# A stack of four low-rank-adapted layers: first weights in pieces, a combined table for the last two layers, and shared last sums

## The chip, the cores and the metric

The kernel runs on one core of a Trainium2 chip. Its time is device microseconds of one execution of the program; three executions are shown, and their median counts. A profile is taken of a separate execution, and its times are microseconds from the start of the span. TensorE (PE) multiplies, VectorE (DVE), ScalarE (ACT) and GpSimd (POOL) do elementwise work, and DMA transfers are issued by SyncE (SP), ScalarE or GpSimd, each on its own queue.

## The reference

The input x has 8 sequences of 256 tokens with 1024 features, in float32. Four residual layers follow each other. Each has low-rank adapters of rank 16, selected per sequence by an index:

```python
# layer 0: x + x W^T + b + 2 * (x A0[i]) B0[i]
# layer 1: gate and up (1024 -> 2752), silu(gate) * up, down (2752 -> 1024),
#          each with an adapter of its own
    Bx = jnp.einsum('bni,bri->bnr', x, B_req)          # layers 2 and 3
    out = jnp.einsum('bnr,bor->bno', Bx, A_req)
    return out * SCALING
    ...
    x = x + _L2_cond_ref(x, L2_cond_A, L2_cond_B, itok_B_4_50)
    x = x + _L3_cond_ref(x, L3_cond_A, L3_cond_B, itok_B_3_7)
```

In layers 2 and 3 nothing but the low-rank part is added, with a factor of 1. With B2, A2, B3, A3 the selected tables of one sequence (the first of each pair going down to rank 16), the output is x + A2 B2 x + A3 B3 (x + A2 B2 x). So it is enough to form t2 = B2 x and t3 = B3 x + (B3 A2) t2, and to add A2 t2 + A3 t3 at the end.

## The kernel before

Activations lie transposed, features on the 128 partitions and tokens along them. The 2048 tokens are worked in two blocks of 1024, a block in two halves (`n`) of 512 tokens, and a half holds two sequences. A chunk is 128 features; x has eight (`NC`), and `arrival` orders them 0, 4, 1, 5, 2, 6, 3, 7. Large products use a seven-product scheme (sums of operands on DVE and GpSimd, seven block products on TensorE, sums of results on DVE), but the first output pair of layer 0 in block 0 is computed plainly, since it can start before any sums (`plain`).

The program is written as units, each a list of products, with hooks in slots before and inside them: `u.before(k, slot, f)` runs `f` k units earlier. Work with a cost can be put in a list, `beside`, which is emptied by shares at the slots of each unit; `need(key)` forces what stands under that key. A scheduler then settles waits and buffers; each engine runs its own instructions in the order in which they were written. Tiles of 8 KB per partition come from one pool of 22 (`big`), PSUM banks from four small pools (`ps_a` two, `ps_b` one, `ps_c` one, `ps_l` four).

**The start.** The kernel issues four small loads of indices (`ids`, L127) and one of the bias (L186) on ScalarE's queue. `load_w(0)` (L782) issues two weight tiles of 512 KB on SP, and `load_x` (L752) the chunks of x, 256 KB each, in turn on SP and ScalarE. DVE works out offsets from the indices (L131 to L202), with which GpSimd gathers adapter tables (L208). `sum_x` makes the sums of x for later units. `plain` (L822) then does, for each half of the tokens, eight chunks times two output tiles, followed by `first_shrink` (x times the gathered A0, L238) and `expand` (L253).

**Layers 2 and 3.** In the last layers each sequence has 16 ranks of layer 2 and 16 of layer 3. In a PSUM bank of 128 rows, rows 64n to 64n+31 hold B2 x and the next 32 rows B3 x, for the two sequences of half n; a mask zeroes, for each token, the ranks of the other sequence. `tables23` gathers the tables in the first unit of the down projection, on TensorE multiplies B3 with A2 (L1271, 16 products that give a 32 by 32 table per half), and places the results in a 128 by 128 table `ba` that is zero elsewhere. `shrink23` (L238) is done in parts, as chunks of the down projection's result become final. `last_layers` then runs shrink of the last chunks, `rank_out` (the mask, L231), the product with `ba` added to the same bank (L1314), `rank_out` again, and eight times two expand products (L1319, by L253), each followed by a DVE sum into the result (L1321) and a store of 256 KB on ScalarE's queue (L1325). In block 0 the stores are put into `beside`; in block 1 they are issued at once.

```python
            t = rank_out(ps, 1.0, f"t2_{blk}")
            nc.tensor.matmul(ps, st["ba"], t, start=False, stop=True, skip_group_check=True)
            t = rank_out(ps, 1.0, f"t23_{blk}")
```

Of the kernel before, what the change touches and what calls it, by code (L numbers as in the profile page):

```python
# [13 lines left out]
P = 128  # L14
# [30 lines left out]

SHARE = {1: 1.1, 2: 0.8, 3: 1.1, 5: 0.7, 6: 0.3, 7: 0.3, 4: 0.8}
SHARE_REST = {1: 0.5, 2: 0.3, 3: 0.5, 5: 0.3, 6: 0.2, 7: 0.2, 4: 0.3}
BIG = 2048
NBIG = 22

# [2 lines left out]
def kernel(  # L53
# [22 lines left out]
    a2s: bass.AP,  # L76
    bb2: bass.AP,
    bb3: bass.AP,
    outT: bass.AP,
):  # L80

# [39 lines left out]
    def bank(pool, name):  # L121
        return pool.tile([P, 512], F32, tag=pool.name, name=name)


    ids = const.tile([P, 4, NB], I32, tag="ids", name="ids")
    for j, tok in enumerate((tok0, tok1, tok2, tok3)):
        nc.scalar.dma_start(out=ids[:, j, :], in_=tok[None, :].to_broadcast([P, NB]))  # L127
    part = const.tile([P, 1], I32, tag="part", name="part")
    nc.gpsimd.iota(part, pattern=[[0, 1]], base=0, channel_multiplier=1)
    part_f = const.tile([P, 1], F32, tag="part_f", name="part_f")  # L130
# [52 lines left out]
        nc.vector.tensor_single_scalar(off_23[rows], off_23[rows], float(SLOTS2 * R), op=ALU.add)  # L183

    bias = const.tile([P, NC], F32, tag="bias", name="bias")
    nc.scalar.dma_start(out=bias, in_=b0)  # L186

# [552 lines left out]
    def layer0(blk):  # L740
        st = sts[blk]

        def load_x():
            st["x"] = xs = [[None] * NN for _ in range(NC)]
            t = {}
            for n in range(NN):
                for h in range(2):
                    t[n, h] = big(f"x_{blk}_{n}_{h}").rearrange("p (c t) -> p c t", c=HC)
                for i, k in enumerate(arrival):
                    xs[k][n] = t[n, k // HC][:, k % HC, :]  # L750
                    at = blk * TB + n * 512
                    (nc.sync, nc.scalar)[i % 2 if blk == 0 else 0].dma_start(  # L752
                        out=xs[k][n], in_=xT[k * P : (k + 1) * P, at : at + 512]
                    )
            st["a0"] = gather_a(a0, 0, blk, f"a0_{blk}")
            st["b0"] = gather_b(bb0, off_b[:, 0, blk : blk + 1], f"b0_{blk}")

# [13 lines left out]
        def x1(k, n):  # L771
            key = "x1", n, k % 2
            if key not in st:
                st[key] = big(f"x1_{blk}_{n}_{k % 2}").rearrange(
                    "p (i c t) -> p i c t", i=2, c=2
                )
            return st[key][:, k // HC, (k // 2) % 2, :]

        def load_w(o):
            t = big(f"w0_{blk}_{o}").rearrange("p (j k) -> p j k", j=2)  # L780
# [30 lines left out]

        def plain(o, at):

            p, x = o + HC, st["x"]
            pss = {}
            at(0)
            for n in range(NN):
                for j in (o, p):
                    pss[j, n] = bank((ps_a, ps_l)[n], f"pp_{blk}_{j}_{n}")
                for i, c in enumerate(arrival):  # L820
                    for j in (o, p):
                        nc.tensor.matmul(  # L822
                            pss[j, n],
                            st["w", o][:, j // HC, c * P : (c + 1) * P],
                            x[c][n],
                            start=i == 0,
                            stop=i == NC - 1,
                        )
# [49 lines left out]
        for i, o in enumerate((0, 2, 1, 3)):  # L878
            if blk == 0 and i == 0:
                u = Unit("0_plain", lambda at, o=o: plain(o, at), 0)  # L880
                u.before(1, 0, lambda o=o: load_w(o))
                u.before(1, 0, load_x)
                for c in range(HC):
                    u.before(1, 0, lambda c=c: sum_x(c))
            else:
                u = Unit(f"0_{blk}_{o}", lambda at, o=o: job(o, at), 1.3)
                u.before(1, 0, lambda o=o: load_w(o))
                u.before(1, 3, lambda o=o: sum_w(o))
                if i == 0:
# [235 lines left out]
    def down_projection(blk):  # L1125
# [133 lines left out]
        def tables23():  # L1259
            st["a23"] = gather_b(a23, off_23[:, blk : blk + 1], f"a23_{blk}")  # L1260
            st["b2"] = gather_a(bb2, 2, blk, f"bb2_{blk}")
            st["b3"] = gather_a(bb3, 3, blk, f"bb3_{blk}")
            a_s = gather_a(a2s, 2, blk, f"a2s_{blk}")


            v, w = (x.rearrange("p b (r c) -> p (b r) c", c=NC) for x in (a_s, st["b3"]))
            ps = bank(ps_l, f"pba_{blk}")
            for c in range(NC):
                for n in range(NN):
# [5 lines left out]
                        start=c == 0,  # L1275
                        stop=c == NC - 1,
                    )
            ba = st["ba"] = const.tile([P, P], F32, tag="ba", name=f"ba_{blk}")
            nc.gpsimd.memset(ba, 0.0)
            for n in range(NN):  # L1280
                rows, at = slice(64 * n, 64 * n + 32), 64 * n + 32
                nc.vector.tensor_scalar_mul(ba[rows, at : at + R], ps[rows, :R], even_f[rows])
                nc.vector.tensor_scalar_mul(
                    ba[rows, at + R : at + 2 * R], ps[rows, R : 2 * R], odd_f[rows]
                )

        def shrink23(chunks):

            for mh in range(2):
                for n in range(NN):  # L1290
                    need(("x2", blk, mh, n))
            if chunks[0] == 0:
                st["p23"] = bank(ps_l, f"p23_{blk}")
            for c in chunks:
# [13 lines left out]
        def last_layers():  # L1308
# [1 line left out]
            x2 = st["x2"]  # L1310
            shrink23([HC - 1, NC - 1])
            ps = st["p23"]
            t = rank_out(ps, 1.0, f"t2_{blk}")
            nc.tensor.matmul(ps, st["ba"], t, start=False, stop=True, skip_group_check=True)  # L1314
            t = rank_out(ps, 1.0, f"t23_{blk}")
            for o in range(NC):
                pss = [bank((ps_l, ps_a)[o % 2], f"p23_{blk}_{o}_{n}") for n in range(NN)]
                for n in range(NN):
                    expand(pss[n], st["a23"], o, t, 64 * n, 64 * n + 64, start=True)  # L1319
                for n in range(NN):  # L1320
                    nc.vector.tensor_add(x2[o][n], x2[o][n], pss[n])  # L1321
# [25 lines left out]
        for o in range(HC):  # L1347
# [4 lines left out]
            if o == 0:  # L1352
# [2 lines left out]
                u.before(1, 4, sum_h)  # L1355
                u.at(0, lambda: need(("hm", blk)))
                u.before(2, 5, tables23)
            else:
                u.at(5, lambda o=o: shrink23([o - 1, o - 1 + HC]))
        units[-1].at(9, last_layers)  # L1360
# [150 lines left out]
```

## Time and profile before

| | us |
|---|---|
| three executions | 1821.07, 1823.34, 1825.03 |
| median | 1823.34 |
| the profiled execution, its own time | 1823.25 |
| its span | 1821.5 |
| TensorE idle before its first product | 9.31 |
| first group of products (L822), from and to | 9.31 to 40.02 |
| start of the last expands (L253), block 1 | 1806.12 |
| last store landed | 1820.37 |

The span runs from the first to the last event that the profiler records. A float32 product is two records on TensorE, one a pass; a pass of 128 by 128 by 512 takes 0.43 us at full clock and 0.855 us at half. The column "granted clock" of a stretch is the mean of what the throttle allowed, 1.00 being full; the whole span has 0.994. The two ends of the span look so in windows (columns: from and to, length, then busy time and number of instructions of PE, PEld, DVE, ACT and POOL, granted clock, share of the 16 DMA engines, GB/s):

```
5.00:10.00 5.00, 0.69 (x1) 0.50 (x2) 0.10 (x2) 0.00 (x0) 0.00 (x0) 1.00 0.73 239
10.00:16.00 6.00, 6.00 (x9) 2.39 (x8) 5.33 (x33) 0.00 (x0) 4.08 (x5) 1.00 0.96 335
16.00:40.00 24.00, 24.00 (x60) 10.33 (x61) 10.18 (x16) 1.28 (x1) 17.85 (x19) 1.00 0.77 274
1806.00:1822.00 16.00, 9.35 (x32) 3.93 (x32) 9.72 (x17) 0.00 (x0) 0.00 (x0) 0.86 0.70 263
```

In the second row nine passes start in 6 us, each twice as long as those of the third row, though the clock column there shows 1.00; the length of the passes is the surer sign at the start.

### The profile page before, as it was taken

The numbers are of one execution on the slowest core, as the hardware profiler recorded it, in microseconds if no ns is written. First come the engines' busy times: TensorE is split into PE (matmuls) and PEld (weight loads), VectorE is DVE, ScalarE is ACT, GpSimd is POOL, SyncE is SP. The second block draws the span as 40 slices with busy tenths as digits, with TensorE's granted clock in tenths as the row PEclk, the third lists the DMA queues.
The fourth block names the chain that finished last, engine by engine and source line by source line (L and its number), as shares of the span: only waits on it lengthen the run. The fifth ranks groups of instructions, "written<-read, shape, count | busy, mean of one in ns | idle before, by whom it ended". The sixth has DMA issues, their size and how long they took to land.

```text
span 1821.5 us, 20497 instructions
## 1 busy us (share of the span) xinstructions
PE 1790.1 (98%) x7588; PEld 1310.4 (72%) x7588; DVE 1081.7 (59%) x1674; ACT 307.0 (17%) x548; POOL 1002.7 (55%) x773
## 2 busy tenths in 40 slices
PE   7999999999999999999899999999999999999998
PEld 3444477878787878788764578888878887888743
DVE  3674354776767575777852464666666668446623
ACT  0111022111111111233310031020202021222100
POOL 5302577887987677334650377675758573444300
PEclk9999999999999999999999999999999999999999
DMA  6376785767675756679741684575757565654302
GB/s 228 144 286 250 268 342 184 301 210 308 244 301 198 273 184 240 236 274 354 264 151 52 231 330 164 201 257 208 254 210 255 211 219 208 228 180 182 110 0 93
DMA packets 114707, 402.33 MB, mean 221 GB/s; under 512 B 12336, under 2 KB 42160, under 8 KB 105136
## 3 DMA queue, kind: packets, MB, share of 16 engines
q1 hardware_dynamic: 97920, 362.84, 54.4%
q0 software_dynamic: 10208, 27.67, 4.4%
q10 hardware_dynamic: 6480, 10.51, 1.6%
q8 instruction: 61, 1.00, 0.2%
q14 instruction: 38, 0.31, 0.0%
HBM read 316.56 MB, written 84.41 MB: 220 GB/s over the span
## 4 chain that ended last, share of the span: by engine, by line
PE 91%; DVE 7%; DMA 1%; issue 1%; ACT 0%; DVEq 0%; SPq 0%; ACTq 0%
PE pa L453 26%; PE pc L453 13%; PE pa L352 10%; PE pa_d L453 9%; PE pb L453 6%; PE pc_d L453 5%; PE pc L352 5%; PE pb L352 3%; PE pb_d L453 2%; PE pl L931 2%; PE pa_r L453 2%; PE pp L822 2%; PE pd L238 1%; PE pc_r L453 1%; PE p L238 1%
## 5 line engine op out<-in xcount | busy, mean ns | idle before, releaser
L453 PE MATMUL pa<-tk,sw 128*128 128x256 f32 x1120 | 268.8, 383 | 1.7 <-DVE c_X L484 1.7
L453 PE MATMUL pc<-tk,sw 128*128 128x256 f32 x1120 | 267.1, 382 | 0.0
L453 PEld LDWEIGHTS pa<-tk,sw 128*128 128x128 f32 x1120 | 209.1, 190 | 58.6 <-issue 11.4
L453 PEld LDWEIGHTS pc<-tk,sw 128*128 128x128 f32 x1120 | 213.9, 191 | 30.9 <-POOL w_B L414 0.8
L453 PE MATMUL pa<-tk,w_B 128*128 128x256 f32 x960 | 228.4, 381 | 0.2 <-DVE c_Y L487 0.2
L453 PEld LDWEIGHTS pa<-tk,w_B 128*128 128x128 f32 x960 | 181.2, 190 | 34.7 <-DVE c_E L484 6.5
L423 POOL TENSOR_TENSOR sw<-w_B 128x512 f32<-128x512 f32 x60 | 77.3, 1289 | 134.6 <-PE pa L453 118.8
L453 PE MATMUL pb<-tk,w_B 128*128 128x256 f32 x480 | 114.5, 382 | 0.0
L453 PE MATMUL pc_d<-dh_d,dw_d 128*128 128x256 f32 x448 | 103.6, 384 | 7.5 <-DVE c_d_X L487 5.7
L591 POOL TENSOR_TENSOR dx_d<-dw_d 128x1024 f32<-128x1024 f32 x14 | 34.5, 2464 | 129.1 <-PE pa L453 44.3
L453 PEld LDWEIGHTS pb<-tk,w_B 128*128 128x128 f32 x480 | 92.3, 192 | 13.0
L453 PE MATMUL pa_d<-dh_d,dw_d 128*128 128x256 f32 x448 | 101.6, 379 | 0.0
L453 PEld LDWEIGHTS pc_d<-dh_d,dw_d 128*128 128x128 f32 x448 | 85.7, 192 | 21.4 <-DVE c_d_X L487 6.1
L484 DVE TENSOR_TENSOR c_X<-c_X,pa 128x512 f32<-128x512 f32 x90 | 61.3, 682 | 64.6 <-PE pa L453 64.6
L414 POOL TENSOR_TENSOR w_B<-w_B,w_B 128x1024 f32<-128x1024 f32 x40 | 93.6, 2363 | 2.4 <-PE pa L453 2.4
L453 PEld LDWEIGHTS pa_d<-dh_d,dw_d 128*128 128x128 f32 x448 | 85.1, 190 | 11.6
L425 POOL TENSOR_TENSOR sw<-w_B 128x512 f32<-128x512 f32 x60 | 85.3, 1422 | 0.0
L426 POOL TENSOR_TENSOR sw<-w_B,sw 128x512 f32<-128x512 f32 x60 | 81.0, 1350 | 3.6
L424 POOL TENSOR_TENSOR sw<-sw,w_B 128x512 f32<-128x512 f32 x60 | 79.2, 1320 | 0.0
L263 ACT ACTIVATE c_X<-pa 128x512 f32<-128x512 f32 x30 | 17.8, 592 | 360.8 <-PE pa L453 360.7
L208 POOL DMA_INDIRECT ad<-in_ad_dram,off_a x48 | 45.9, 957 | 37.8 <-PE pd L238 27.1
L592 POOL TENSOR_TENSOR dw_d<-dw_d,db_d 128x1024 f32<-128x1024 f32 x14 | 34.4, 2460 | 45.4 <-DVE dk_d L321 12.6
(363 smaller groups left out, 3191.9 us busy)
## 6 DMA issues: line engine op xcount, KB each, us to landing
tk<-toks SPq DMA_DIRECT2D x140, 896.0 KB, 6.9
w_B<-in_wgu_dram SPq DMA_DIRECT2D x40, 1024.0 KB, 6.0
tk_r<-toks SPq DMA_DIRECT2D x28, 896.0 KB, 9.9
hk<-c_Z SPq DMA_DIRECT2D x32, 512.0 KB, 4.8
dh_d<-hk SPq DMA_DIRECT2D x14, 1024.0 KB, 7.5
hk<-c_Y SPq DMA_DIRECT2D x24, 512.0 KB, 3.7
w<-in_w_dram SPq DMA_DIRECT2D x16, 512.0 KB, 7.2
x1d<-x SPq DMA_DIRECT2D x8, 1024.0 KB, 6.8
```

The lines of the kernel that those rows point to most:

```text
L208: nc.gpsimd.indirect_dma_start(out=t, out_offset=None, in_=table, in_offset=bass.IndirectOffsetOnAxis(ap=off, axis=0),)
L238: nc.tensor.matmul(ps[32 * r : 32 * r + 32, :], v, src, start=start, stop=stop, skip_group_check=True)
L352: nc.tensor.matmul(ps, v[j], m[j], start=start and k == 0, stop=k == len(moving) - 1, skip_group_check=True,)
L414: f(self.raw[out][:, c], self.raw[a][:, c], self.raw[b][:, c])
L423: nc.gpsimd.tensor_add(s1, m21, m22)
L424: nc.gpsimd.tensor_sub(s2, s1, m11)
L425: nc.gpsimd.tensor_sub(s3, m11, m21)
L426: nc.gpsimd.tensor_sub(s4, m12, s2)
L453: nc.tensor.matmul(ps[:, q, :], w(j, q, kk), tok(j, kk), start=start and q == 0 and kk == 0, stop=kk == self.deep - 1, skip_group_check=True,)
L484: nc.vector.tensor_add(view(out, r, k), view(old, r, k), ps)
L822: nc.tensor.matmul(pss[j, n], st["w", o][:, j // HC, c * P : (c + 1) * P], x[c][n], start=i == 0, stop=i == NC - 1,)
L931: nc.tensor.matmul(ps[outs], st["bgu", g][rows, table, n, cols], st["t"][rows, table, n, :], start=True, stop=True, skip_group_check=True,)
```

## The change

Three things are changed. First, the start: the weights of the first output pair are loaded in four pieces (`load_piece`), each issued just before the chunk of x that it meets and on the same queue: chunk 0 alone, chunks 1 to 3, chunk 4 alone, chunks 5 to 7. The small loads of indices and bias move from ScalarE's queue to GpSimd's. DVE fills a tile with zeros first of all, and `plain` begins with three products of it into a bank that nothing reads. Second, the product with `ba` in `last_layers` goes. Since t3 = (B3 + B3 A2 B2) x, the table B3 is itself replaced: a new input `b23` holds the tables B2 and B3 by rows of rank, one more gather fetches the rows, `table3` multiplies them with the 32 by 32 tables (16 products, each with 32 rows of `rows_b` as the stationary operand), and DVE adds the result to the gathered B3 before the first `shrink23`. Third, in the last block four of the sixteen last sums (n = 1 of output chunks 0, 2, 4, 6) are done by a ScalarE copy out of PSUM and a GpSimd sum.

```diff
+TAIL = (0, 2, 4, 6)
+WARM = 3
...
+    zero = big("zero")[:, :512]
+    nc.vector.memset(zero, 0.0)
+    ps_zero = bank(ps_b, "ps_zero")
...
-        nc.scalar.dma_start(out=ids[:, j, :], in_=tok[None, :].to_broadcast([P, NB]))
+        nc.gpsimd.dma_start(out=ids[:, j, :], in_=tok[None, :].to_broadcast([P, NB]))
...
-    nc.scalar.dma_start(out=bias, in_=b0)
+    nc.gpsimd.dma_start(out=bias, in_=b0)
...
-                    (nc.sync, nc.scalar)[i % 2 if blk == 0 else 0].dma_start(
-                        out=xs[k][n], in_=xT[k * P : (k + 1) * P, at : at + 512]
-                    )
+                    q = (nc.sync, nc.scalar)[i % 2 if blk == 0 else 0]
+                    if blk == 0 and n == 0 and i < 4:
+                        load_piece(q, k)
+                    q.dma_start(out=xs[k][n], in_=xT[k * P : (k + 1) * P, at : at + 512])
...
+        def load_piece(q, k):
+
+            if ("w", 0) not in st:
+                st["w", 0] = big(f"w0_{blk}_0").rearrange("p (j k) -> p j k", j=2)
+            c = slice(k, k + 1 if k % HC == 0 else k + HC - 1)
+            q.dma_start(
+                out=st["w", 0][:, :, c.start * P : c.stop * P].rearrange(
+                    "p j (c m) -> p j c m", m=P
+                ),
+                in_=w0[0 : HC + 1 : HC, :, c, :].rearrange("j p c m -> p j c m"),
+            )
...
+            for _ in range(WARM):
+                nc.tensor.matmul(ps_zero, zero[:, :P], zero, start=True, stop=True)
...
-                u.before(1, 0, lambda o=o: load_w(o))
                 u.before(1, 0, load_x)
...
+            rows_b = big(f"b23_{blk}")[:, :D]
+            gather(rows_b, b23, off_23[:, blk : blk + 1])
...
-            ba = st["ba"] = const.tile([P, P], F32, tag="ba", name=f"ba_{blk}")
-            nc.gpsimd.memset(ba, 0.0)
+            ba = const.tile([P, 2 * R], F32, tag="ba", name=f"ba_{blk}")
...
+                nc.vector.tensor_scalar_mul(ba[rows, :R], ps[rows, :R], even_f[rows])
+                nc.vector.tensor_scalar_mul(ba[rows, R:], ps[rows, R : 2 * R], odd_f[rows])
+            st["b3_rows"] = rows_b, ba
+
+        def table3():
+
+            rows_b, ba = st.pop("b3_rows")
+            pss = [bank(ps_l, f"pbb_{blk}_{n}") for n in range(NN)]
+            for c in range(NC):
+                for n in range(NN):
+                    rows = slice(64 * n, 64 * n + 32)
+                    nc.tensor.matmul(
+                        pss[n][:, c * 2 * R : (c + 1) * 2 * R],
+                        rows_b[rows, c * P : (c + 1) * P],
+                        ba[rows],
+                        start=True,
+                        stop=True,
+                        skip_group_check=True,
+                    )
+            for n in range(NN):
+                v = st["b3"].rearrange("p b (r c) -> p (b r) c", c=NC)
+                v = v[:, 2 * n * R : 2 * (n + 1) * R]
+                new = pss[n][:, : NC * 2 * R].rearrange("p (c r) -> p r c", c=NC)
+                nc.vector.tensor_add(v, v, new)
...
+            need(("b3", blk))
...
-            t = rank_out(ps, 1.0, f"t2_{blk}")
-            nc.tensor.matmul(ps, st["ba"], t, start=False, stop=True, skip_group_check=True)
             t = rank_out(ps, 1.0, f"t23_{blk}")
+            if blk + 1 == NBLK:
+                spare = big("spare").rearrange("p (j t) -> p j t", j=4)
...
-                    nc.vector.tensor_add(x2[o][n], x2[o][n], pss[n])
+                    if blk + 1 == NBLK and o in TAIL and n == 1:
+
+                        copy(spare[:, TAIL.index(o)], pss[n])
+                        nc.gpsimd.tensor_add(x2[o][n], x2[o][n], spare[:, TAIL.index(o)])
+                    else:
+                        nc.vector.tensor_add(x2[o][n], x2[o][n], pss[n])
...
+                u.before(1, 5, lambda: queue(("b3", blk), (0.9, table3)))
```

More of the change, by code (lines that the diff above doesn't have):

```diff
@@ L78 @@
     bb3: bass.AP,
+    b23: bass.AP,
     outT: bass.AP,
@@ L1277, in tables23 @@
                     )
-            ba = st["ba"] = const.tile([P, P], F32, tag="ba", name=f"ba_{blk}")
-            nc.gpsimd.memset(ba, 0.0)
+            ba = const.tile([P, 2 * R], F32, tag="ba", name=f"ba_{blk}")
             for n in range(NN):
[L1281 to L1285, printed above, removed]
+                rows = slice(64 * n, 64 * n + 32)
[7 more added lines that the diff above has]
+                for n in range(NN):
+                    rows = slice(64 * n, 64 * n + 32)
+                    nc.tensor.matmul(
[11 more added lines that the diff above has]
+                nc.vector.tensor_add(v, v, new)
         def shrink23(chunks):
@@ L1488 @@
         "bb3": _shrink(np, g["L3_cond_B"].transpose(0, 2, 1)),
+        "b23": np.concatenate([expands(g[f"L{i}_cond_B"]) for i in (2, 3)]),
     }
```

## The prediction

> **What bounds the kernel now.** I read four views in this order. First the page's busy table and its chain of waits:
>
> ```profile
> PE 1790.1 (98%) x7588; PEld 1310.4 (72%) x7588; DVE 1081.7 (59%) x1674; ACT 307.0 (17%) x548; POOL 1002.7 (55%) x773
> PE 91%; DVE 7%; DMA 1%; issue 1%; ACT 0%; DVEq 0%; SPq 0%; ACTq 0%
> ```
>
> TensorE is busy for 98% of the span and is 91% of the chain. DVE's 7% and the 1% of DMA are what a rearrangement can recover, so I looked for their places. The chain in order of time shows two, the start and the end (columns: start us, us, what):
>
> ```profile
> 0.75 0.40 SPq L782
> 1.70 7.47 DMA x<-in_xT_dram
> 9.31 30.71 PE pp L822 x64
> 40.02 3.60 PE t L238 x32
> ...
> 1803.46 0.70 DVE t L231
> 1804.21 1.14 PE p L1314 x2
> 1805.37 0.70 DVE t L231
> 1806.12 1.18 PE p L253 x4
> 1807.30 0.67 DVE c_d_E L1321
> ...
> 1815.74 0.60 DVE c_d_X L1321
> 1816.33 0.60 DVEq L1506
> ```
>
> At the start TensorE waits 9.31 us for the first x chunk, queued on SP behind two 512 KB weight loads. At the end comes a chain shrink, mask, small product, mask, expand, and then 16 sums on DVE, 0.60 us apart. The end of the execution, though, is a store:
>
> ```profile
> GB/s 0 0 0 0 0 0 0 0 0 0 0 0 0 0 0 0 339 391 380 387 372 380 380 380 384 387 387 372 380 384 395 376 380 384 372 402 30 0 0 0
> out_dram<-c_d_Y ACTq DMA_DIRECT2D x4, 256.0 KB, 3.1
> ```
>
> That is the DMA view of 1800 to 1822 in slices of 0.55 us. From 1808.8 to 1819.8 the output moves at a flat 380 GB/s. 4 MB at that rate are 11 us against 16 x 0.60 = 9.6 us of sums: the sums are not the tighter limit. The last sum starts at 1816.25, its store is issued at 1817.40, and the data lands at 1820.37.
>
> **The start.** Removed: the wait. The first product now needs a 128 KB piece of weights and 256 KB of x on SP, with as much on the ACT queue beside it: 768 KB in place of 1.25 MB on SP alone. The old start moved about 1.04 MB by 6.75 us (its DMA row sliced at 1.13 us: 8, 85, 249, 207, 378 GB/s), so 768 KB are there at about 5.9 us, and I put the first x at 5.9 to 6.9.
>
> Added: three products of zeros, six passes. They wait for one more 128x512 memset on DVE (the mask's takes 0.48 from 0.93), so they run from 1.5. The timeline of the old first products has weight loads 0.855 us apart from 10.29 to 15.40, then 0.43 apart: half clock for 6.06 us, full after. Six cold passes end near 6.75, as the data comes.
>
> Here the row and the Trainium skill differ ("TensorE: Matmul & The Clock Gate", Part 1): the activity window is 3.4 us and free-running. TensorE then needs one full busy window, between 3.4 and 6.8 us of work, 5.1 in the mean; the row gives 6.06. From 1.6 there are 70 passes (the 64 of the chain's line, two to a product, and six): 70 x 0.43 = 30.1, plus half the cold time, 3.03 by the row or 2.56 by the rule. The first group of products ends at 34.7 or 34.3, where before it ended at 40.02. I take the middle, -5.5, and 0.4 for a gap between the zeros and the data: **-5.1**. Ends: -3.5 (data 2 us late) and -6.5 (warm after 3.4 us). If zeros warmed nothing, only the earlier data would be left, about -2.5.
>
> Moved queues: ids and bias go from ACT to GpSimd ahead of the gathers, five issues of 0.55 to 0.78 us each as GpSimd's other loads; on ACT they held x back until 5.67. DVE now has the sums of x ahead of the offsets, which shifts the first gathers from 10.7 to about 15.7 and the landing of the last one that the shrink needs from 23 to 28; the shrink comes at about 34.4, the expand's table (landed 26.3 before, some 31 now) is used at 38. Cover remains, so nothing; without it each us late is a us.
>
> **The table.** Removed per block: the small product and one masking, 1803.46 to 1805.37 = 1.91 us at the end, and 1.85 at the end of block 0 (from 1019.48). Added per block: 16 matmuls of 32 rows, two row groups in turn, 32 passes in the middle of the last down-projection unit, where TensorE is the bound, so each counts whole. The trace has no such shape. Nearest below is the small table product:
>
> ```profile
> L1271 PE MATMUL pba<-bb,a2s 128*32 128x32 f32 x64 | 2.5, 239 | 0.0
> L1314 PE MATMUL p<-t,ba 128*128 128x512 f32 x4 | 2.2, 624 | 0.8 <-DVE t L231 0.8
> L263 ACT ACTIVATE c_X<-pa 128x512 f32<-128x512 f32 x30 | 17.8, 592 | 360.8 <-PE pa L453 360.7
> L729 POOL TENSOR_TENSOR wo<-wo 128x512 f32<-128x512 f32 x8 | 10.2, 1271 | 23.3 <-DMA wo<-in_wd_dram 23.2
> ```
>
> Its 32 passes lie in 1.22 us of timeline (the 239 overlap), 38 ns each, but load only 32 columns. The new ones load 128 columns, which elsewhere takes 108 to 145 ns for a pair. The skill's "TensorEngine Tiling (Array Packing)", Instruction Overhead, gives a flat 60 cycles for a small product and says nothing against it: by the rule or the 38 ns row the table costs 1.24, gain 0.65 a block. By the load of weights with two row groups side by side it is 16 x 0.108 to 0.145 = 1.7 to 2.3; if row groups take turns, 32 x 0.145 = 4.6, with transitions 4.9. I take 2.2, since the load is what differs from the 38 ns row: 2 x 2.2 - 1.91 - 1.85 = **+0.65**, ends -1.3 and +6. Two sums on DVE and one more gather a block lie beside TensorE's work; the products wait for that gather, which is issued well ahead, behind the sums of the weights. The gathered tile and the zeros take two of the 22 buffers; of the loads that change buffers I found none whose former user ends later: 0. GpSimd's memset of the small table goes, worth nothing.
>
> **The last sums.** Four of 16 go to ScalarE (copy, 0.592) and GpSimd (sum, 1.271). Gain, at best: DVE ends 2.4 us earlier, but the 380 GB/s hold the end, so the floor is -1.0. Price: the stores are issued by ScalarE too, in order. Each pair of output chunks puts there a copy (0.59, then 0.08), three free stores and one that waits for GpSimd's sum. Behind that waiting store stand the next two stores and the next copy. So one round is 0.59 + 0.08 + 1.27 + 0.05 and about three issues of 0.34 to 0.44 that aren't under the wait, 3.1 to 3.35 us, against 4 stores x 0.60 = 2.4 before. From the first expand, the old last landing is 14.25 us later (1806.12 to 1820.37). New: first copy at 2.2, four rounds to 14.75, and 2.2 for an unqueued store: 16.95. **+2.7**, ends +1.7 and +3.7 (and -1.0 if nothing queued). In block 0 four passes of the next product move into the time that was paced by DVE; 0.
>
> **Sum.** 1823.25 is the profiled execution (span 1821.5), beside a median of 1823.34, so they serve alike. -5.1 + 0.65 + 2.7 = -1.75: **1821.5**. A change under 0.2% (3.65 us) can't be told from none here: the three runs lie 4 us apart, and the trace holds five stretches of half clock (274.8, 291.9, 885.8, 1073.5, 1090.6, each 3.41 us, 1.7 lost), four of them after the 2.9 us of 32-row products at L931; a shift against the free-running window can drop or add one. Hence +-2.5 for this case.
>
> **Rivals.** *Faster, chance 0.38.* The start gives its end (-6.5 with data in time), the table costs 1.24 (-1.3 both), the tail 1.7: -6.1, 1817. For it: weight loads overlap products everywhere in this trace. Against: ScalarE's order alone costs more than the table can give.
>
> *Slower, 0.18.* The table's narrow products run one after the other, 4.9 us a block, and like the products of L931 leave a window so idle that the clock halves after it: 2 x (4.9 - 1.88 + 1.7) = +9.4, with -5.1 and +2.7 +7.0: 1830. It decides above 3.2 us a table (with that halving). For it: four of four such stretches at L931 were followed by half clock. Against: the 64-row expands start 7 ns apart in two row groups, so groups do overlap.
>
> *The zeros do nothing, inside the rest.* The clock stays half until 6 us of real products are done: -2.5 + 0.65 + 2.7 = +0.9, 1824; no measurable change. The old first products were real, and the same number of passes; nothing shows that zeros count less, so it is a small part of my 0.44.
>
> Forecast with this last one 0.44. Slower than 1827.0 has 0.18; faster than 1819.7 the faster case, 0.38; the rest 0.44. Range: 1814.5 to 1827.5 takes in most of the faster case with two stretches of half clock fewer; the likeliest case alone is 1819 to 1824.
>
> **What would show it.** Start: the first product of real data before 7 us, full clock by 6.8, first group ended at 34 to 35.5. Table: 32 passes in 1.7 to 2.5 us twice, no half clock behind. Tail: ScalarE's copies about 3.2 us apart, stores bunched behind GpSimd's sums, the DMA row no longer flat, and 16 to 17.5 us from first expand to last landing. I am wrong if GpSimd's sum is much slower than 1.3 us, if ScalarE issues the stores past a waiting one, or if zero products leave the clock low.

## The result and the profile after

The changed kernel is slower: 1838.68 us median of six runs (1830.58 to 1845.17) against 1822.8 of six runs of the kernel before (1821.07 to 1825.03). The ratio is 1.0083, interval [1.0056, 1.0109]. The profiled execution took 1845.17 us, its span 1843.4, so it is the longest of the six, and of its 21.9 us above the span before some six are its own luck.

The busy table of the changed kernel, then its chain of waits at the start and at the end (start us, us, what):

```profile
PE 1799.8 (98%) x7654; PEld 1318.0 (72%) x7654; DVE 1084.7 (59%) x1673; ACT 309.7 (17%) x552; POOL 1013.6 (55%) x782
```

```profile
0.74 3.09 DMA w<-in_w_dram
3.83 0.02 issue
3.85 8.54 DMA x<-in_xT_dram
12.39 0.03 issue
12.42 28.75 PE pp L845 x60
41.18 3.60 PE t L245 x32
...
1819.66 2.04 PE p L260 x8
...
1829.39 1.26 POOL c_d_Y L1368
1830.65 2.04 issue
1832.69 1.30 POOLq L1557
```

TensorE is busy for 9.7 us more. The passes that came and went make about 6 of them (an estimate: 4.3 for the zeros and 2 x 1.9 for the tables, less 2 x 1.1 for the small products); the rest is the same work at half clock. The first group of products ends at 41.18, later than before (40.02), because the chunk of x that is needed second landed at 12.29, and because TensorE, which had come to full clock with the zeros, was at half clock behind that wait (columns as in the windows of before):

```profile
6.00:8.00 2.00, 1.94 (x4) 0.63 (x4) 0.00 (x0) 0.00 (x0) 0.00 (x0) 1.00 1.13 231
12.40:18.00 5.60, 5.58 (x7) 2.50 (x8) 0.28 (x2) 1.28 (x1) 0.00 (x0) 0.50 0.99 335
```

The chain's 60 passes take 28.75 us, where 60 times 0.43 are 25.8: the lost clock is 2.95 of the start. And at the end stands an entry of GpSimd's sequencer where a DVE sum stood: line L1557 is the end of the program, and what GpSimd does there is a drain, the closing instruction that every engine has there; the trace has GpSimd's from 1832.69 to 1842.58. The last store had landed at 1837.28.

The same products of the two traces, set side by side, give the place of each microsecond (after minus before, profiled executions):

| up to | difference, us | what came in |
|---|---|---|
| end of the first group, 40 | +1.2 | the start |
| 360 | -0.3 | |
| 480 | +4.8 | waits at 366.7 and 465.3, a window of half clock |
| 810 | +7.0 | short waits, a window of half clock |
| 900 | +15.2 | waits of 3.5 at 836 and 7.6 (5.7 before) at 893, half clock behind both |
| 945 | +17.3 | the table, block 0 |
| 1022 | +15.5 | the small product and its mask are gone |
| 1720 | +15.4 | half clock fallen otherwise, the table of block 1 |
| 1806 | +13.6 | the small product is gone |
| end | +21.9 | the last sums, +8.35 |

So in this profile the start gave nothing, the tail cost 8.35, the table half a microsecond, and more than half of the loss, 12 us, lies in the middle, where the change touches nothing. A later profile of the same kernel (the repeat, c_after below, 1834.86 us) has the same tail (8.4) and table, but a start of -1.8 and 4.5 in the middle: there the tail is most of the loss. The view of TensorE's waits of the changed kernel names them (engine line waited for: us in total, times, longest):

```profile
PE pc_d L460 <- DVE c_d_X L494: 7.6, 1, 7.6
PE pp L845 <- DMA x<-in_xT_dram: 4.8, 2, 4.5
PE pc_d L460 <- DVE c_d_Z L494: 3.5, 1, 3.5
...
PE pa L460 <- DVE c_X L494: 1.7, 1, 1.7
```

Only one of the three waits for DVE was there before, at 5.7.

### The profile page after: what moved, and what is told of

Same layout as the page of the kernel before. It is cut to its first block, busy times and chain, and to the rows that moved or that the text cites. A ratio compares the mean times of both kernels' runs of the same rounds, so it can differ in the third digit from the quotient of the medians.

```text
span 1843.4 us, 20658 instructions
## 1 busy us (share of the span) xinstructions
PE 1799.8 (98%) x7654; PEld 1318.0 (72%) x7654; DVE 1084.7 (59%) x1673; ACT 309.7 (17%) x552; POOL 1013.6 (55%) x782
## 4 chain that ended last, share of the span: by engine, by line
PE 90%; DVE 7%; DMA 2%; issue 1%; SPq 0%; ACT 0%; POOL 0%; POOLq 0%; ACTq 0%; DVEq 0%
PE pa L460 25%; PE pc L460 12%; PE pa L359 10%; PE pa_d L460 9%; PE pb L460 6%; PE pc L359 5%; PE pc_d L460 5%; PE pa_r L460 3%; PE pb L359 2%; PE pl L953 2%; PE pb_d L460 2%; PE pp L845 2%; PE pc_r L460 1%; PE pd L245 1%; DMA dk_d<-hk 1%
## 5 line engine op out<-in xcount | busy, mean ns | idle before, releaser
L460 PEld LDWEIGHTS pa<-tk,sw 128*128 128x128 f32 x1120 | 210.4, 191 | 59.1 <-issue 13.7
L460 PE MATMUL pc_d<-dh_d,dw_d 128*128 128x256 f32 x448 | 106.4, 392 | 12.8 <-DVE c_d_X L494 7.6
L460 PEld LDWEIGHTS pa_d<-dh_d,dw_d 128*128 128x128 f32 x448 | 85.5, 191 | 11.8
L359 PE MATMUL pa<-ht,wd 128*128 128x512 f32 x128 | 59.1, 594 | 0.0
```

What stands on the lines that cost most here:

```text
L359: nc.tensor.matmul(ps, v[j], m[j], start=start and k == 0, stop=k == len(moving) - 1, skip_group_check=True,)
L460: nc.tensor.matmul(ps[:, q, :], w(j, q, kk), tok(j, kk), start=start and q == 0 and kk == 0, stop=kk == self.deep - 1, skip_group_check=True,)
```

## The experiments

The runs came from several chips. On most, the kernel before had a median of 1823 to 1826; on two (that of a_notail, b_poolend, a_oldstart and a_oldtable, and that of b_warm6, b_warm6_sw and b_best) it had 1848 and 1849. On both, the profiles show TensorE held up at the first adapter products until about 60 us or later; I call these the chips with the long wait (the expectations speak of late gathers). What held TensorE is not shown. The packets of the first nine gathers were over as early there as elsewhere (27.19 us in b_poolend, 27.17 in the kernel before), but many records of their landing are missing (294 and 864 records of DMA landings up to 45 us). The wait moves with the gathers all the same: in all seven of these profiles, DVE's mask behind it starts 52 to 54 us after the first gather is issued. So each run is compared with the runs of the kernel before beside it, and stretches of the trace with the same stretch.

### The tail: a chain and a drain

The changed kernel without shared sums, the kernel before with one GpSimd copy behind the last sum, and the changed kernel with the first shared sum alone:

```diff
# a_notail
-TAIL = (0, 2, 4, 6)
+TAIL = ()
# b_poolend, on the kernel before
+                    if blk + 1 == NBLK and o == NC - 1 and n == 1:
+                        last = const.tile([P, 1], F32, tag="last", name="last")
+                        nc.gpsimd.tensor_copy(last, x2[o][n][:, :1])
# a_tail0, on the changed kernel
-TAIL = (0, 2, 4, 6)
+TAIL = (0,)
```

> The changed kernel with all sixteen last sums on DVE again (start and table as changed). Theory (closing drain): in the changed kernel's profile GpSimd's last instruction, a drain, ends 8.6 us after its last sum and 5 us after the last store has landed, so the four sums cost about 5.0 (drain) + 3.4 (stores issued late) = 8.4 us: median near 1830. Rival (only ScalarE's order of copies and stores costs): 3.4 us less than the changed kernel, near 1835.

> The kernel before, with one GpSimd copy of a single column behind the very last sum and nothing else. Closing drain theory: the last sum ends at about 1816.9 of the span, the drain about 8.6 to 9 us later, so the span ends near 1826.5 in place of 1821.5: +5 us, median near 1828. Rival: a GpSimd instruction of 0.1 us beside the stores costs nothing, median near 1823.

> The changed kernel with only the first of the four shared sums left (n = 1 of chunk 0), the other three on DVE. From the first of the last expands to the end of the span the changed kernel takes 23.7 us and the kernel before 15.35. Closing drain theory: GpSimd's only sum ends about 4.3 us after the first expand, its drain about 9 us later, at 13.3, ahead of the last store: the stretch is 15.3 to 16.5 us, so 7 to 8.4 us are gone with three of four sums. Rival (each shared sum costs its share of the 8.4): 17.5 us.

Measured: the copy of one column, 0.18 us of work, cost 4.6 us (1852.26 against 1847.65; ratio 1.0020 [1.0008, 1.0032]). GpSimd's drain ran from 1847.02 to 1855.49 and the span ended at 1856.3 (a line of its chain, one of its timeline):

```profile
1847.02 0.21 POOLq L1509
1847.05 0.18 POOL L1324 COPY last<-c_d_Y 128x1 f32<-128x1 f32 x1 [95.42 <-DVE c_d_Y L1321]
```

The drain is in every trace, and ends 8.3 to 8.6 us after the end of GpSimd's last work. In the kernel before it runs from 1720.58 to 1729.60, behind work that ended at 1721.34, and under TensorE's. It costs nothing until GpSimd's last work ends later than about 8.5 us before the last store lands (an estimate from these figures). Why it takes so long no trace shows.

From the first of the last expands to the end, the changed kernel took 23.71 us, and 23.72 on another chip; without shared sums 17.0; the kernel before 15.35. So of the 8.35, the shared sums are 6.7 and 1.65 are there without them. With only the first shared sum it took 18.44: its drain ended 12.87 us in, ahead of the last store at 17.15, so nothing of the 18.44 is drain, as the drain theory said. But the number it gave, at most 16.5, was missed, and the rival's 17.5 was nearer: its last store was issued only 0.5 us later after the first expand than before, and landed 2.4 us later after that. Uneven stores, which come below, account for 1.65 of this where no sum is shared; the rest is open. In medians, the kernel without shared sums stood 14.5 above before on its chip (1.0079 [1.0055, 1.0103]); 9.9 of that are the long wait (see the start), so its forecast of 1830 can't be held against this median, and the changed kernel itself did not run there. The one with a single shared sum stood 6.2 above (1.0033 [1.0016, 1.0049]).

The chain that was forecast is there too. This is the timeline of the changed kernel's tail (start us, us, engine line what):

```profile
1828.71 0.60 ACT L270 ACTIVATE spare<-p 128x512 f32<-128x512 f32 x1 [2.76 <-DVE c_d_Y L1370]
1829.39 1.26 POOL L1368 TENSOR_TENSOR c_d_Y<-c_d_Y,spare 128x512 f32<-128x512 f32 x1 [2.08 <-ACT spare L270]
1830.68 0.82 ACTq L1374 DMA_DIRECT2D out_dram<-c_d_Y  x2
1831.60 0.41 ACTq L1374 DMA_DIRECT2D out_dram<-c_d_X  x1
1832.06 0.60 ACT L270 ACTIVATE spare<-p 128x512 f32<-128x512 f32 x1 [2.75 <-DMA out_dram<-c_d_X]
```

One round from copy to copy is 3.35 us, three stores wait behind GpSimd's sum, and the last store was issued 14.80 us after the first expand.

### The start, and what it does to the gathers

```diff
# a_oldstart, on the changed kernel: ids and bias on ScalarE as in a_ids, and
-                    if blk == 0 and n == 0 and i < 4:
-                        load_piece(q, k)
+                u.before(1, 0, lambda o=o: load_w(o))
-            for _ in range(WARM):
-                nc.tensor.matmul(ps_zero, zero[:, :P], zero, start=True, stop=True)
# a_oldtable, on the changed kernel: ba of 128 by 128 again, no b23, no table3
+            t = rank_out(ps, 1.0, f"t2_{blk}")
+            nc.tensor.matmul(ps, st["ba"], t, start=False, stop=True, skip_group_check=True)
-                u.before(1, 5, lambda: queue(("b3", blk), (0.9, table3)))
# c_after: the changed kernel itself
# a_ids, on the changed kernel
-        nc.gpsimd.dma_start(out=ids[:, j, :], in_=tok[None, :].to_broadcast([P, NB]))
+        nc.scalar.dma_start(out=ids[:, j, :], in_=tok[None, :].to_broadcast([P, NB]))
-    nc.gpsimd.dma_start(out=bias, in_=b0)
+    nc.scalar.dma_start(out=bias, in_=b0)
# b_warm8, on the kernel before: the memset of the zeros, and
+WARM = 8
+            for _ in range(WARM):
+                nc.tensor.matmul(ps_zero, zero[:, :P], zero, start=True, stop=True)
# a_pieces8: zeros (3), ids on ScalarE, TAIL = (), the old table, eight pieces of one chunk
-                    if blk == 0 and n == 0 and i < 4:
+                    if blk == 0 and n == 0:
-            c = slice(k, k + 1 if k % HC == 0 else k + HC - 1)
+            c = slice(k, k + 1)
```

> The changed kernel with the start of before (weights in two loads ahead of x, indices and bias on ScalarE's queue, no zeros). The start itself lost 1.1 us in the profile of the changed kernel. If the further 6 to 12 us in the middle (new waits of TensorE for DVE at 366, 836 and 893, each with half clock behind it) come from the shift of the start, this kernel loses none of them: near 1831. If they come from the table's buffers and gathers, it stays near 1837.5.

> The changed kernel with the product with ba in last_layers in place of table3 (start and tail as changed). The table alone costs 2.2 us a block and saves 1.9: near 1838 if the waits in the middle have another cause; near 1832 if the table's gather and buffers cause them.

> The changed kernel itself, on the chip of the three kernels that go with it. If the gathers are as quick here as in the first profiles (the table of layer 0 landed 4 to 10 us after its issue), 10 to 16 us above the kernel before. If they are as late as on the chip of the four earlier runs, where TensorE waited for them until 62 us with the start of before and until 72 us with the changed one, about 25 us above.

> The changed kernel with the loads of indices and bias on ScalarE's queue as before (pieces, zeros, table and tail as changed). Theory (late offsets): the first gather is issued at 11 to 14 us of the span in place of 20.2, since the offsets no longer stand behind a sum of x that waits for the second half; on a chip with late gathers this gives back up to 9 us against the changed kernel, on a chip with quick ones nothing. Rival (the pieces alone delay the start): as the changed kernel in both cases. The fifth chunk of x lands at about 12 us still if the pieces cause that, at 9 to 10 if the index loads do.

> The kernel before with eight products of zeros ahead of the first group, nothing else. 16 passes from 1.5 us, at half clock until about 6.8, end near 9.3 when x lands, so the first group runs at full clock from the start: it ends near 37 in place of 40.0, 3 us less. If any shift of the start costs in the middle as it did in the changed kernel, 0 to 5 us more than before instead.

> The kernel before with a start of its own: indices and bias on ScalarE's queue as before, three products of zeros, and the first weights in eight pieces of 128 KB, each ahead of the chunk of x that it meets, so that no piece of 384 KB stands before the second chunk. Theory (the two pieces of 384 KB hold the second chunk back until 12.3): the fifth chunk lands by 9 us, TensorE waits under 1.5 us after the zeros, the first group ends near 35.5, and the kernel is 3 to 5 us under the one before. Rival (rows of 512 bytes are slow as such, or the index loads are in the way): the second chunk comes after 11 us again and nothing is gained.

| run | median | before beside it | ratio, interval | first group ended |
|---|---|---|---|---|
| old start | 1855.91 | 1847.65 | 1.0036 [1.0020, 1.0052] | not compared |
| old table | 1872.02 | 1847.65 | 1.0119 [1.0098, 1.0140] | not compared |
| the change again | 1839.25 | 1826.47 | 1.0073 [1.0050, 1.0096] | 38.18 |
| ids on ScalarE | 1835.21 | 1826.47 | 1.0058 [1.0033, 1.0083] | 37.79 |
| eight products of zeros | 1824.84 | 1826.47 | 0.9993 [0.9981, 1.0005] | 38.28 |
| eight pieces | 1830.45 | 1826.47 | 1.0017 [1.0005, 1.0030] | 39.95 |

The zeros do what was hoped as long as the data follows them. With eight of them the clock is full at the first real product, and the overshoot (they end at 10.65, the data was there at 9.1) is all that is wrong; with six, in a later run, the group ended at 36.98. Neither kernel was measurably faster for it. The pieces are the weak part. In the changed kernel the first x came at 5.85, as forecast, but the second at 12.29 (12.06 on the other chip), while the transfers ran at a third of their later rate, as the DMA view of the first 45 us shows (slices of 1.13 us):

```profile
GB/s 0 37 233 132 310 342 166 128 125 292 383 408 348 268 339 317 366 351 382 397 402 426 419 412 422 324 135 47 189 313 62 58 58 58 58 58 47 51 33 58
```

From 6.8 to 10.1 us they moved 125 to 166 GB/s. With the index loads back on ScalarE the second chunk landed at 9.88, as the theory of the index loads had it; but the waits then came later (1.55 us at 13.7), the group ended only 0.4 us earlier, and the medians are not told apart. The theory isn't settled either: b_best_pieces, further down, has the same loads in the same order, and its second chunk came at 11.67. Eight small pieces did not cure it: the second chunk came at 12.13, so the rival of that run was right, and TensorE waited 3.3 us (1.4 of this kernel's 4.0 us above before are the uneven stores of its tail, 16.79 us long). In seven profiles TensorE waited 2.5 to 4.6 us for the second chunk. Five have half clock behind the wait, and the group ends at 39.49 to 41.18; two, with 3.2 and 3.34 us, have not, and it ends at 38.18 and 37.97. Whole weights with six products of zeros beat all the pieces: 36.98 and, beside b_best_pieces with 39.49 (37 to 38 was expected), 37.34.

The larger price of the changed start appears on the chips with the long wait. The first gather was issued at 20.24 us with the changed start, at 10.70 before and at 9.19 with the loads on ScalarE: with the changed start its offsets stand, on DVE, behind a sum of x that waits for the second half of x (until 17.73). On a chip with the long wait, that shift is passed on in full: DVE's mask before the expand waited until 72.3 with the changed start (no shared sums) and until 62.4 with the old one. On the chips of the result the gathers were done in time (33.97, where the expand began at 45.8). The cover was there on one chip and gone on another.

The kernel with the old start stood 6 us under the one without shared sums, although it has the drain, and 16 us under the one with the old table; 9.9 of each are this wait. It stood 8.3 above before, and its last stretch alone is 8.5 longer (23.82 against 15.35): the table costs nothing measurable with the start of before, and nothing of the loss of the middle is left in its median. That is what the run's first theory, the shift of the start, said (8 above before). The run with the old table was the slowest of all, so the table's gather and buffers aren't the cause. But on this chip the long wait stands between the start and the middle, so the two runs don't show how the shift works.

### The middle: sums that meet

The kernel before with six products of zeros, then the sums of layer 0's last weights emitted earlier, then also the sums of the down projection's rank rows emitted later:

```diff
# b_warm6: WARM = 6 on the kernel before
# b_warm6_sw: that, and
-                u.before(1, 3, lambda o=o: sum_w(o))
+                u.before(1, 0 if blk == 1 and i == 3 else 3, lambda o=o: sum_w(o))
# b_best, b_best_2: that, and
-                u.before(3, 4, rank_rows)
+                u.before(2, 4, rank_rows)
```

> The kernel before with six products of zeros ahead of the first group (12 passes, ending near 9.3, as x lands) and nothing else. The first group ends near 37, 3 us earlier than before. In the kernel with eight such products the gain of the start was taken back at 195 us, where DVE's sums of layer 0's last weights (0.69 us each alone) took 1.8 to 2.4 us beside GpSimd's sums and TensorE waited 2.7 us. If that is where the start's gain goes, the wait is there again, 2 to 3 us, and the median is within 2 us of before. If the wait was chance, the median is 3 us under before.

> The same, and the sums of the last weights of layer 0 are emitted three slots earlier, so that DVE does them near 171 us, before GpSimd begins its sums at 186. Contention theory: the four sums take 0.7 us each, TensorE's wait near 195 is gone, and the start's 3 us survive until at least 360: 1.5 to 3 us under the kernel with the six products alone. Rival (TensorE waits there for something that comes at a fixed time, a transfer): the wait stays.

> The same again, and the sums of the down projection's rank rows (DVE, six sums that take 12 us beside GpSimd's sums of weights near 877 to 889, while TensorE waits 5.7 to 7 us, with half clock behind it) are emitted one unit later. If TensorE's wait there comes from those sums standing ahead of the sum that it needs, the wait shrinks below 2 us and a window of half clock goes: 5 to 8 us under the kernel without this edit. If other work of DVE takes their place, or the sums are late for the next unit, nothing is gained.

> The kernel before with six products of zeros and the two groups of DVE sums moved, again, as the measure for the three that go with it and on another chip if it is one. 15.4 us from the first of the last expands to the end, stores at a flat 380 GB/s; 4 to 13 us under before.

With six products the first group ended at 36.98, 3 us earlier, and the kernel was not faster: 1850.95 against 1849.06 (1.0012 [0.9997, 1.0027]). On this chip the long wait swallows the 3 us: TensorE is held up until 64 us here, and until 66 with the start of before in b_poolend, on another chip with the long wait. Beside that profile, this one was 2.4 us ahead at 40 us, 0.7 behind from 70 to 214 and 4.5 behind at 220. On a chip without the long wait, the eight products kept 1.7 us until 194 and had lost them by 220 (+0.5). The same sums stand at both places, here near 210:

```profile
210.35 2.18 DVE L347 TENSOR_TENSOR sw<-w 128x512 f32<-128x512 f32 x1
210.70 1.28 POOL L733 TENSOR_TENSOR wo<-wo 128x512 f32<-128x512 f32 x1
212.33 0.75 POOL L731 DMA_DIRECT2D wo<-in_wd_dram  x1 [0.36 <-issue]
212.57 2.37 DVE L348 TENSOR_TENSOR w<-w 128x512 f32<-128x512 f32 x1
...
218.42 0.74 DVE L801 SCALAR_TENSOR_TENSOR x<-pa,bias,x 128x512 f32<-128x512 f32 x1
...
219.21 2.05 PE L356 MATMUL pa<-xt,sw 128*128 128x512 f32 x3 [2.70 <-DVE x L801]
```

A DVE sum of two SBUF tiles takes 0.69 us alone, and 2.18 and 2.37 here while GpSimd sums. In the whole trace of the kernel before, 134 such sums of 128x512 without a GpSimd sum beside them take 0.67 to 0.74; of the 79 that have one for over 60% of their time, half take more than 1.14 and the longest 4.12. The 1208 with an operand in PSUM take 0.67 to 0.70, with GpSimd or without. GpSimd pays too: a sum of its own that starts while such a DVE sum runs takes 1.71 (the median of 63), others 1.27. TensorE waits for the sum that stands behind them, 2.70 us. With DVE's sums emitted earlier they ran here:

```profile
190.49 0.74 DVE L347 TENSOR_TENSOR sw<-w 128x512 f32<-128x512 f32 x1 [4.14 <-DMA w<-in_w_dram]
191.27 0.69 DVE L348 TENSOR_TENSOR w<-w 128x512 f32<-128x512 f32 x1
```

and TensorE's wait was gone: 1846.48, 4.5 us under the kernel with the zeros alone (0.9984 [0.9969, 0.9998] of before). Moving the rank rows too gave 1836.05 (0.9940 [0.9921, 0.9959]), and on another chip 1814.37 against 1826.12 (0.9951 [0.9933, 0.9968]): TensorE's wait of 5.7 to 7 us near 885 and the half clock behind it are gone, more than the 5 to 8 us that I expected (in the profiles, about 7.5 us near 910). A move takes the sums out of GpSimd's time and also from ahead of the sum that TensorE needs; which of the two counts for more, no run separates.

The changed kernel loses in the same way at other places. The same sum of the two traces near 364, before and then after:

```profile
363.55 1.15 DVE L496 TENSOR_TENSOR c_Y<-c_Y,c_X 128x512 f32<-128x512 f32 x1
364.62 0.67 DVE L487 TENSOR_TENSOR c_X<-c_X,pa 128x512 f32<-128x512 f32 x1
365.17 1.29 POOL L423 TENSOR_TENSOR sw<-w_B 128x512 f32<-128x512 f32 x1
365.32 4.12 DVE L496 TENSOR_TENSOR c_Y<-c_Y,c_X 128x512 f32<-128x512 f32 x1
```

```profile
363.49 1.28 POOL L430 TENSOR_TENSOR sw<-w_B 128x512 f32<-128x512 f32 x1
363.63 4.14 DVE L503 TENSOR_TENSOR c_Y<-c_Y,c_X 128x512 f32<-128x512 f32 x1
...
367.69 0.67 DVE L494 TENSOR_TENSOR c_X<-c_X,pa 128x512 f32<-128x512 f32 x1
...
368.42 1.99 PE L460 MATMUL pa<-tk,w_T 128*128 128x256 f32 x8 [1.73 <-DVE c_X L494]
```

GpSimd's sums came 1.7 us earlier. So the long sum is no longer the one behind the sum that TensorE needs (`c_X<-c_X,pa`), but the one ahead of it: 1.15 us have become 4.14, and TensorE waits. The order of the instructions is the same; only the phase of two engines differs. This is what the Trainium skill states ("GPSIMD Engine Reference", Specifications: the SBUF interfaces are shared with VectorE, with contention for DVE instructions with two SBUF inputs). The trace agrees and adds the size: 0.69 against up to 4.1 for a 128x512 sum with two SBUF inputs, and no change for one with a PSUM operand.

The changed kernel's other waits have such sums ahead of them too, at 465 one of 4.15 us, and at 836 four in a row that would take 2.8 us at 0.69 each:

```profile
831.05 7.81 DVE L1168 TENSOR_TENSOR c_d_E<-c_d_E,x 128x512 f32<-128x512 f32 x4
838.79 0.67 DVE L494 TENSOR_TENSOR c_d_Z<-c_d_Z,pc_d 128x512 f32<-128x512 f32 x1
839.61 2.78 PE L460 MATMUL pc_d<-dh_d,dw_d 128*128 128x256 f32 x8 [3.50 <-DVE c_d_Z L494]
```

At 893 they are the sums of the rank rows.

### The last stores, and the changed kernel mended

> The same with the changed kernel's extra input b23, which nothing reads. If the place of the output in memory makes the last stores slow, they dip below 340 GB/s here and the last stretch is 16.8 us or more; if not, 15.4 us as without it.

> The kernel of the first run with the first weights in the changed kernel's four pieces (indices and bias on ScalarE's queue, three products of zeros, no extra input). If the pieces make the last stores slow, the last stretch is 16.8 us or more; if the extra input does, 15.4 us. At the start the pieces gain about as much as the whole weights with six products of zeros: the first group ends between 37 and 38.

> The changed kernel (pieces, zeros, table) with indices and bias on ScalarE's queue, all last sums on DVE and the two groups of sums moved. If the loss in the middle is DVE's sums beside GpSimd's, TensorE's waits near 195 and 890 are gone and the kernel stands within 3 us of the first run (0.6 for the table, 1.5 for the last stores), below before. If the middle loses for another reason, it stays 5 us or more above the first run.

```diff
# b_best_in: b_best, and an input that no instruction reads
+    b23: bass.AP,
# b_best_pieces: b_best, and
-WARM = 6
+WARM = 3
+                        load_piece(q, k)
# a_best: the changed kernel with ids and bias as in a_ids, the two groups as in b_best, and
-TAIL = (0, 2, 4, 6)
+TAIL = ()
```

The transfers of the last 20 us (slices of 0.5 us), first of the kernel without the extra input, then of the one with it:

```profile
GB/s 0 0 0 0 0 0 0 352 389 377 389 365 365 393 389 377 373 393 389 365 385 393 389 369 381 393 385 385 373 37 0 0 0 0 0 0 0 0 0 0
```

```profile
GB/s 0 0 0 0 0 0 0 348 385 324 299 377 324 340 242 270 369 410 406 406 266 291 393 393 406 397 320 332 389 340 234 143 4 0 0 0 0 0 0 0
```

The last stretch was 15.39 and 16.81 us. The extra input alone, unread, makes the stores uneven and 1.4 us longer. The other profiles without shared sums agree: 15.34 to 15.44 without the input, 16.71 to 17.0 with it. The one exception, the pieces without the input (16.48), began its last expands at half clock (1797.1 to 1800.5), which made the first sums late; its rate was flat but for one dip there. That the output then lies elsewhere in memory is the likely reason, but only argued.

Medians, all beside 1826.12: 1814.37 without either, 1815.51 with the input (0.9942 [0.9917, 0.9966]), 1815.30 with the pieces (0.9942 [0.9921, 0.9963]). And the changed kernel with its table, pieces and zeros, but without shared sums, with the index loads on ScalarE and the two groups moved: 1813.24, 0.9938 [0.9917, 0.9959]. No run told these four apart. It is below the kernel before by 12.9 us, where the change as made was 12.8 above in the repeat and 15.9 in the result. In its profile the waits near 195 and 890 are gone; one of 3.8 at 828 is left. But the kernel before gains as much, within the noise, from zeros and the two moves alone (1814.37), so none of the gain is shown to be the change's. The changed kernel with its tail and index loads put back and the sums left where they were did not run; what each of the three edits gave is not separated.

## Why the prediction was wrong

The terms of the sum, in us, beside what the two profiles of the changed kernel show against the profile of before:

| term | predicted | first profile | repeat |
|---|---|---|---|
| start | -5.1 | +1.2 | -1.8 |
| table | +0.65 | +0.55 | +0.5 |
| last sums | +2.7 | +8.35 | +8.4 |
| middle | 0 +-2.5 | +11.8 | +4.5 |
| sum | -1.75 | +21.9 | +11.6 |

Three steps failed: the end of the last sums, the arrival of data at the start, and a middle that was put at nothing.

- **The last sums.** The step that failed is the end of the program, which the prediction took to be the landing of the last store; GpSimd's drain was a term put at nothing. It ended 5.3 us beyond the last store, and one GpSimd copy alone cost 4.6. It was in the trace before, at 1720.58, under other work; I had read GpSimd's durations, not what its engine does at the end of the program. The chain itself is right: rounds of 3.35 us, and the last store issued 14.80 us after the first expand, against 14.75. Its landing came at 17.6 in place of 16.95; the stores are 1.4 us longer with the extra input alone, so that is the likely reason.
- **The start.** The zeros behaved as reckoned (full clock at the first real product or just behind it), and the first x landed at 5.85, where 5.9 to 6.9 was forecast. The step that failed is the data behind the first chunk. The sum let the products run on from there, with 0.4 us for one gap, but the second chunk landed at 12.29 (12.06 in the repeat), and TensorE waited 4.5 us (3.2), once with the clock halved behind it. Index loads that landed at 12.1 and not 9.8, and pieces of 384 KB, were ahead of it; which of them counts stays open, since the same loads gave 9.88 and 11.67. The 6.06 us of cold time that the prediction set against the skill's rule lie inside the 3.4 to 6.8 that it estimated from that rule, so the two did not differ there.
- **The gathers.** The first was put at 15.7 and came at 20.24. That the cover held where the result was taken is luck: on another chip it cost 9.9 us.
- **The middle.** The +-2.5 held the half clock alone and no new wait between the start and the tail, and the -5.1 was taken to reach the end. For what is late next, the prediction looked at gathers and at buffers that come free late, not at two engines that slow each other where their phase shifts. The two profiles lost 12 and 4.5 us there; in the first, the four waits that were followed (366.7, 465, 836 and 893) all stand behind DVE sums beside GpSimd's, with half clock after three of them. That these sums cause TensorE's waits is shown on the kernel before, by the moves; for the changed kernel it rests on the traces and on a_best, which changed more. With the sums moved, its table and pieces no longer lose, but they don't gain either (1813.24 against 1814.37 without them).
- **The table.** Right: its 32 passes ran in pairs about 0.11 us apart, 1.9 us from first to the next product, against 2.2, with 1.75 to 1.9 saved. The slower rival (4.9 us a table) fell with this.

## What to carry to other kernels

Before giving GpSimd work at the end, look for its drain in the trace: where its last work ends less than about 8.5 us before the last store lands, the drain sets the end. Where two engines share SBUF, a kernel bound by TensorE hangs on their phase: look for DVE sums of two SBUF tiles that take two or three times their shortest time ahead of a sum that TensorE waits for, and move them to a stretch in which GpSimd transfers or waits. And a wait at the start can be filled rather than removed: warming products brought the first group's end 3 us forward and disturb no queue, though the kernel gained from it only once the next waits were gone too.

## What was not expected of the hardware

GpSimd's closing drain ended 8.3 to 8.6 us after its last work in every trace. On two of the chips TensorE was held up until 62 to 72 us at the products of the first gathers, though their packets moved as early as elsewhere, and the hold moved with the issue of the first gather; its cause is open. And an input that no instruction reads changed the rate of the last stores from 380 GB/s to one between 242 and 410, 1.4 us in all.
